# Layer 0 of a two-layer mixer: the transposed copy of x from a second load in runs of 32 channels, turned on VectorE

## The chip, the cores and the metric

The kernel runs on one core of a Trainium2 chip. The metric is device time in microseconds, the median of several runs. Beside the runs there is one profiled execution, from which all rows of the profile come; it has a time of its own. Engines are called PE (TensorE), DVE (VectorE), ACT (ScalarE), POOL (GpSimd) and SP (SyncE, whose queue issues nearly all DMAs here).

## The reference

The input x has 128 rows of 256 tokens of 256 channels, fp32. Two layers are applied, each to a group-normalised x (32 groups of 8 channels, mean and variance over all tokens), and added to x. Layer 0 is attention along the tokens of a row, with 8 heads of 32 channels, a bias b from a second input z that is the same for all rows, and a gate; layer 1 is attention with 4 heads within a band of 16 tokens. Cut to layer 0:

```python
g = _gn(x)                                   # group norm: mean and variance of each of 32 groups
m_norm = layer_norm(g)                       # over the channels of a token
q, k, v = m_norm @ Wq.T, m_norm @ Wk.T, m_norm @ Wv.T
b = (layer_norm(z) @ Wb.T)                   # one value per head and pair of tokens
gate = sigmoid(g @ Wg.T + bg)                # from g itself, not from m_norm
p = softmax(q @ k.T / sqrt(32) + b)
x = x + ((p @ v) * gate) @ Wo.T + bo
```

So layer 0 needs x twice with the channels on the partitions: as g for the gate, and as m_norm for q, k and v.

## The kernel before, in words

The work has three stages. The first reads all of x for the moments of the groups and all of z for the bias, whose exponential stays in SBUF (`eb`). It is a loop over 16 blocks of z with a hand-written plan (`plan`, `mark`) that slips the first steps of layer 0 in at quarters of blocks: `norm` makes the rows M0 and R0 (mean and reciprocal deviation of each channel, the same on all partitions) and centres pair 0, `weigh` takes its token moments, `now.turn` transposes it.

The second stage is layer 0, a loop over 64 pairs of rows; each pass handles steps of several pairs: `now` is in its scores, `nxt` is being prepared, `nn` is normalised, `was` and `old` are being finished. The third stage is layer 1, a loop over pairs as well.

Within a stage the order of each engine's instructions is the order in which they are written (`tc.manual_schedule()`), and each engine takes its own in order. Waits come from data and from buffers: pools with a number of buffers for each tag, PSUM tiles of the tag "s" (two buffers of 2 banks) for scores and for the transposes, and "mm" (two of one bank) for projections, values and output rows.

One pair passes through these steps; the lines are those of the profile:

- `__init__` (L1225, SP): loads xt, the pair with tokens on the partitions. It is made three pairs ahead.
- `centre` and `scale` (L1233, L1236, POOL): xg = (xt - M0) * R0, for `nn`.
- `moments`, `root`, `send`, `fetch` (L1246 to L1264): the layer norm's factor of each token, sent to DRAM in `rs_d` and fetched back as rs_r, a row repeated on all partitions.
- `turn` (L1274 on PE, L1278 on ACT): eight 128x128 transposes of xg into a PSUM tile of the tag "s", and two copies into xgT, channels on partitions.
- `normal` (L1283, POOL): xnT = xgT * rs_r. The layer norm's mean is taken out in the weights.
- `project` (L1296, L1300): gT from xgT (a tanh; the half that a sigmoid needs is in the weights), qT and kT from xnT. `values` (L1311, L1317): v from xnT.
- `scores` (L1330, L1337): keys times queries into two tiles of "s", and exp on ACT in place.
- `add_bias` (L1346 on DVE, L1351 on POOL): e = exp(scores) * eb, and the key sums eboth, which add the two halves of the keys.
- `apply` (L1362, L1370): e times v into ps_ov, and the sums of e into ps_su. `gate` (L1377): oT = (gT + 1) * ps_ov. `invert` (L1383 to L1391): 1/ps_su, sent to DRAM and fetched as rvb. `normalize` (L1407, POOL): oT * rvb.
- `out_row`, `keep_row` (L1417 to L1430): the output projection and the sum with xt; every four pairs eight rows of the new x go to DRAM, and their group moments for layer 1 are taken on DVE (L1445).

A pass of the loop has four rounds of scores. In the second, `nn` is scaled and gT of `now` is projected; in the third, `now.apply(0)` stands ahead of `nxt.turn()`, so that the transposes come between the sums (L1370) and `now.values(1)`; `nxt.normal()` follows the key sums of the third round on POOL. In the fourth round qT and kT of `nxt` are projected from xnT.

Layer 1 gets its transposed x in another way: a second load of x whose runs are 32 channels, four DMAs for a pair (L1720, xs), and one block transpose on DVE (L1730), then a bias on ACT (L1735).

Of the kernel before, what the change touches and what calls it, by code (L numbers as in the profile page):

```python
# [9 lines left out]
F32 = mybir.dt.float32  # L10
AF = mybir.ActivationFunctionType
ALU = mybir.AluOpType
# [4 lines left out]
P = 128  # L17
# [4 lines left out]
def bcast(ap, axis, n):  # L22

    ap = ap.unsqueeze(axis)
    shape = list(ap.shape)
    shape[axis] = n
    return ap.broadcast_to(shape)
# [746 lines left out]
def fast_kernel(  # L774
# [25 lines left out]
    nc = tc.nc  # L800
    S, I, C = x.shape
    CZ = z.shape[2]
    H = wbT.shape[1]
    D0 = C // H
# [3 lines left out]
    NB = I // P  # L808
    KC = C // P
    NP = S // 2  # L810
    N2 = 2 * I
# [4 lines left out]
    const = ctx.enter_context(tc.tile_pool(name="const", bufs=1))  # L816
    dram = ctx.enter_context(tc.tile_pool(name="dram", bufs=1, space=DRAM))

    ident = const.tile([P, P], F32, name="ident")
# [111 lines left out]
    for a in range(KC):  # L931
        for h in range(H1):
            n = P // H1
# [5 lines left out]
    for h in range(H1):  # L939
        n = P // H1  # L940
# [57 lines left out]
    def mm(name):  # L998
        return ps_mm.tile([P, 512], F32, name=name, tag="mm")
# [199 lines left out]
    HQ = P // D0  # L1199
    NT = 2 * NB  # L1200
# [11 lines left out]
    for n in range(RC):  # L1212
# [2 lines left out]
            bcast(ident.rearrange("p (q d) -> p q d", q=HQ)[:, :, n * D0 // RC], 2, D0),  # L1215
        )

    class Pair:


# [7 lines left out]
            )  # L1228


        def centre(self):
            self.xg = la.tile([P, NT, C], F32, name="xg", tag="xg", bufs=2)
            nc.gpsimd.tensor_tensor(self.xg, self.xt, bcast(M0, 1, NT), ALU.subtract)  # L1233

        def scale(self):
# [226 lines left out]
    def some(n):  # L1462
        for _ in range(min(n, len(later))):
            later.pop(0)()
# [10 lines left out]
    def pair(p):  # L1475
        return Pair(p) if p < NP else Nobody()
# [20 lines left out]
    def norm():  # L1497
        nonlocal M0, R0, nxt
        M0, R0 = next(steps)
        now.centre()  # L1500
        now.scale()
        nxt = pair(1)

    def weigh():
# [5 lines left out]

    plan = {
        (0, 4): begin, (1, 1): lambda: next(steps), (1, 3): lambda: next(steps), (1, 4): take, (2, 3): norm,
        (3, 4): weigh,
        (5, 3): lambda: now.send(nc.scalar),
# [13 lines left out]
    behind, nx, n = None, 0, 0  # L1528
# [39 lines left out]
    su = ps_o.tile([P, I], F32, name="ps_su")  # L1568

    with tc.manual_schedule():  # L1570
        old = was = Nobody()
        es = nn3 = None
        for p in range(NP):

            nxt.root()
            nxt.send()
            e0 = now.add_bias(0, 0, now.scores(0, 0))
            was.apply(1, es)
            was.gate(1)
            was.invert()  # L1580
            nxt.fetch()
            nn.centre()
            if p == 0:
                nxt.residual()
            now.project("qT", 1)
            now.project("kT", 1)
            some(1 if p < NP - 2 else 3)
            now.values(0)
            now.keep_values(0)

            es = e0, now.add_bias(0, 1, now.scores(0, 1))
            nn.scale()
            if p == 0:
                now.residual()
            for m in range(KC):
                now.project("gT", m)
            old.out_row(1)
            some(1 if p < NP - 2 else 3)
            old.keep_row(1)

            nn3 = pair(p + 3)
            e0 = now.add_bias(1, 0, now.scores(1, 0))
            now.apply(0, es)
            now.gate(0)
            nxt.turn()
            nxt.normal()
            was.normalize(0)
            now.values(1)
            now.keep_values(1)
            nn.moments(0)  # L1610
            if p == NP - 1:
                some(8)

            es = e0, now.add_bias(1, 1, now.scores(1, 1))
            was.normalize(1)
            nn.residual()
            nxt.project("qT", 0)
            nxt.project("kT", 0)
            nn.moments(1)
            some(3 if p < NP - 2 else 9)  # L1620
            was.out_row(0)
            was.keep_row(0)
            old, was, now, nxt, nn = was, now, nxt, nn, nn3
        was.apply(1, es)
        was.gate(1)
        was.invert()
        old.out_row(1)
        was.spread()
        old.keep_row(1)
        for r in range(2):  # L1630
            was.normalize_last(r)
        for r in range(2):
            was.out_row(r)
            was.keep_row(r)
        some(len(later))
# [29 lines left out]
    with tc.tile_pool(name="l1", bufs=2) as sb, tc.tile_pool(  # L1665
        name="l1s", bufs=4
    ) as sm, tc.tile_pool(name="ps1_mm", bufs=2, space=PSUM) as ps_mm, tc.tile_pool(
        name="ps1_s", bufs=1, space=PSUM
    ) as ps_s, tc.tile_pool(name="ps1_o", bufs=1, space=PSUM) as ps_o:

        def mm1(name):
            return ps_mm.tile([P, 512], F32, name=name, tag="mm")
# [174 lines left out]
        def pair1(p):  # L1847
            return Pair1(p) if p < NP else Nobody()
# [15 lines left out]
        with tc.manual_schedule():  # L1864
            now, nxt = pair1(0), pair1(1)
# [18 lines left out]
        with tc.manual_schedule():  # L1884
            was = Nobody()
            for p in range(NP - 1):
                nn = pair1(p + 2) if p == 0 else n3
# [27 lines left out]
                was, now, nxt = now, nxt, nn  # L1915
# [19 lines left out]
        ps = mm1("ok_ps")  # L1935
# [4 lines left out]
@with_exitstack  # L1940
def mixer_kernel(ctx, tc, *args):

    nc = tc.nc
    keep = ctx.enter_context(tc.tile_pool(name="verdict", bufs=1))
    verdict = keep.tile([1, 1], mybir.dt.int32, name="verdict")
    fast_kernel(tc, *args, verdict)
    again = nc.values_load(verdict[0:1, 0:1], min_val=0, max_val=1)
    with tc.If(again > 0):
        general_kernel(tc, *args)
# [53 lines left out]
```

## Time and profile before

| | |
|---|---|
| runs | 3310.61 us median of 3 (3309.5 to 3310.71) |
| profiled execution | 3316.03 us, its span 3314.3 us |
| busy, share of the span | PE 95%, DVE 64%, POOL 59%, ACT 44% |
| first stage | 0 to about 240 us |
| layer 0 | about 240 to 2090 us, PE busy 599.85 of the 600 us from 300 to 900 |
| layer 1 | from about 2098 us on |
| share of time that the DMA engines are busy | 0.23 from 300 to 900 us, 0.38 from 2110 to 3300 us |

The matmuls of PE overlap, and their ends are modelled, so a busy PE says less than the chain does: the chain of work that ended last is followed back from the last instruction, at each step to what released it, or to the instruction before it on its engine. Where it runs through one engine alone, that engine sets the pace there. An fp32 matmul appears as two records in most rows. A row of the timeline can stand for several instructions of one kind (xN), and its length is then from the first start to the last end.

### The profile page before, as it was taken

What the parts mean: (1) busy time and instruction counts of PE and PEld (TensorE: products, weight loads), DVE (VectorE), ACT (ScalarE), POOL (GpSimd) and SP (SyncE); (2) the same over time, 40 slices, a digit from 0 to 9 for tenths busy, and PEclk for the clock granted to TensorE, in tenths of its full rate; (3) what the DMA queues carried; (4) which work ended last, traced back from release to release, by engine and by line L of the source; (5) the groups of instructions that cost most, each with busy time, mean ns of one, the idle gap of its engine ahead of it and who ended that gap; (6) DMA issues with size and microseconds to landing.
All of it is one profiled execution on the core that took longest, in us unless ns stands there. A gap on an engine that the chain in (4) does not pass through costs nothing.

```text
span 3314.3 us, 80768 instructions
## 1 busy us (share of the span) xinstructions
PE 3157.9 (95%) x34656; PEld 1977.2 (60%) x34656; DVE 2121.6 (64%) x3179; ACT 1452.7 (44%) x2121; POOL 1962.8 (59%) x1375
## 2 busy tenths in 40 slices
PE   5389999999999999999999999699999999999998
PEld 3255555555555555555555555466666666666666
DVE  7955666666666666666666666466655555555566
ACT  2264444444444444444444444244444444444443
POOL 2378777777787777787887776233333333333332
PEclk8699999999999999999999999899999999999999
DMA  9951212212221222222122211533333434343431
GB/s 354 375 137 43 75 49 75 75 46 65 72 75 49 75 75 60 64 64 69 49 75 75 75 49 52 104 79 91 85 90 86 92 85 91 85 92 84 92 90 54
DMA packets 464879, 295.92 MB, mean 89 GB/s; under 512 B 312480, under 2 KB 413728, under 8 KB 463360
## 3 DMA queue, kind: packets, MB, share of 16 engines
q1 hardware_dynamic: 459440, 287.76, 31.7%
q8 instruction: 275, 4.51, 0.6%
q10 hardware_dynamic: 5072, 2.90, 0.3%
q14 instruction: 92, 0.75, 0.1%
HBM read 221.85 MB, written 68.75 MB: 88 GB/s over the span
## 4 chain that ended last, share of the span: by engine, by line
PE 91%; DVE 3%; DMA 3%; ACT 1%; POOL 1%; SPq 1%; issue 0%; ACTq 0%; POOLq 0%; DVEq 0%
PE ps_p L1296 21%; PE ps_p L1745 14%; PE ps_sc L1330 8%; PE ps_y L1833 7%; PE ps_ov L1362 7%; PE ps_v L1760 7%; PE ps_y L1417 7%; PE ps_v L1311 6%; PE ps_o L1802 3%; PE ps_su L1370 3%; PE ps_sc L1774 3%; PE ps_x L1274 2%; PE ps_su L1802 1%; DVE st L1178 1%; DVE zst L1103 1%; DMA zt<-in_z_dram 1%
## 5 line engine op out<-in xcount | busy, mean ns | idle before, releaser
L1351 POOL TENSOR_TENSOR eboth<-e 128x512 f32<-128x512 f32 x512 | 640.6, 1273 | 392.9 <-DVE e L1346 389.7
L1346 DVE TENSOR_TENSOR e<-ps_sc,eb 128x1024 f32<-128x1024 f32 x512 | 603.1, 1219 | 307.0 <-ACT ps_sc L1337 306.9
L1337 ACT ACTIVATE ps_sc<-ps_sc 128x1024 f32<-128x1024 f32 x512 | 492.8, 1006 | 509.2 <-PE ps_sc L1330 509.2
L1784 POOL TENSOR_TENSOR e<-e,bw 128x384 f32<-128x384 f32 x256 | 259.5, 1035 | 769.8 <-ACT e L1782 769.8
L1745 PE MATMUL ps_p<-xgT,w_in 128*128 128x512 f32 x1024 | 470.3, 602 | 4.5 <-issue 3.7
L1745 PEld LDWEIGHTS ps_p<-xgT,w_in 128*128 128x128 f32 x1024 | 190.1, 191 | 203.7 <-issue 174.8
L1330 PE MATMUL ps_sc<-qT,kT 32*128 32x256 f32 x4096 | 293.3, 400 | 2.1 <-ACT kT L1300 2.1
L1296 PE MATMUL ps_p<-xnT,wq 128*128 128x512 f32 x512 | 267.3, 634 | 3.5 <-POOL xnT L1283 3.1
L1833 PE MATMUL ps_y<-w_out,oT 128*128 128x256 f32 x1024 | 250.3, 388 | 2.6 <-DVE oT L1818 2.6
L1837 DVE TENSOR_TENSOR yo<-ps_y,xt 128x512 f32<-128x512 f32 x128 | 88.4, 690 | 251.9 <-PE ps_y L1833 149.7
L1362 PE MATMUL ps_ov<-e,v 128*32 128x256 f32 x4096 | 247.7, 382 | 0.0
L1417 PE MATMUL ps_y<-wo,oT 128*128 128x256 f32 x1024 | 242.1, 379 | 2.0 <-POOL oT L1407 1.2
L1417 PEld LDWEIGHTS ps_y<-wo,oT 128*128 128x128 f32 x1024 | 194.3, 190 | 82.5 <-issue 59.3
L1311 PE MATMUL ps_v<-wv,xnT 128*128 128x256 f32 x1024 | 242.2, 379 | 0.0
L1330 PEld LDWEIGHTS ps_sc<-qT,kT 32*128 32x128 f32 x4096 | 184.9, 184 | 94.4 <-issue 83.6
L1296 PE MATMUL ps_p<-xnT,wk 128*128 128x512 f32 x512 | 240.8, 592 | 0.0
L1296 PE MATMUL ps_p<-xgT,wg 128*128 128x512 f32 x512 | 236.8, 605 | 0.0
L1760 PE MATMUL ps_v<-w_in,xgT 128*128 128x256 f32 x1024 | 231.8, 379 | 0.0
L1815 DVE RECIPROCAL rv<-odd 128x256 f32<-128x256 f32 x128 | 224.4, 1753 | 4.4
L1760 PEld LDWEIGHTS ps_v<-w_in,xgT 128*128 128x128 f32 x1024 | 194.4, 190 | 53.5 <-issue 30.1
L1317 DVE TENSOR_TENSOR v<-ps_v,vb_r 128x512 f32<-128x512 f32 x128 | 88.6, 692 | 206.8 <-PE ps_v L1311 206.8
L1311 PEld LDWEIGHTS ps_v<-wv,xnT 128*128 128x128 f32 x1024 | 189.6, 190 | 50.8 <-issue 31.0
(169 smaller groups left out, 4989.9 us busy)
## 6 DMA issues: line engine op xcount, KB each, us to landing
xa<-in_x_dram SPq DMA_DIRECT2D x8, 4096.0 KB
xt<-in_x_dram SPq DMA_DIRECT2D x64, 512.0 KB
x<-xo SPq DMA_DIRECT2D x16, 2048.0 KB
xs<-x SPq DMA_DIRECT2D x256, 128.0 KB
xt<-x SPq DMA_DIRECT2D x64, 512.0 KB
rvb<-rsum SPq DMA_DIRECT2D x252, 128.0 KB
out_dram<-yo SPq DMA_DIRECT2D x63, 512.0 KB
zt<-in_z_dram SPq DMA_DIRECT2D x15, 2048.0 KB
```

Of the source, the lines that this page charges most:

```text
L1296: nc.tensor.matmul(ps, w[:, k, m * P : (m + 1) * P], getattr(self, src)[:, k, :], start=(k == 0), stop=(k == KC - 1),)
L1311: nc.tensor.matmul(self.ps_v[:, b * C : (b + 1) * C], self.xnT[:, k, t * P : (t + 1) * P], wv[:, k, :], start=(k == 0), stop=(k == KC - 1),)
L1330: nc.tensor.matmul(self.pss[q // 2][:, q % 2, b, :], self.kT[rs, c, r * I + b * P : r * I + (b + 1) * P], self.qT[rs, c, r * I : (r + 1) * I],
L1337: nc.scalar.activation(self.pss[a], self.pss[a], AF.Exp)
L1346: nc.vector.tensor_tensor(e, pss[a], eb[:, h : h + 2], ALU.mult)
L1351: nc.gpsimd.tensor_tensor(t, es[a][:, :, 0, :], es[a][:, :, 1, :], ALU.add)
L1362: nc.tensor.matmul(ov[q * D0 : (q + 1) * D0, c, :], self.v[:, r, b, h * D0 : (h + 1) * D0], es[q // 2][:, q % 2, b, :], start=(b == 0), st ...
L1417: nc.tensor.matmul(self.ps_y[:, b * C : (b + 1) * C], self.oT[r][:, k, b * P : (b + 1) * P], wo[:, k, :], start=(k == 0), stop=(k == KC - 1),)
L1745: nc.tensor.matmul(ps, w_in[:, k, n * C + m * P : n * C + (m + 1) * P], self.xgT[:, k, :], start=(k == 0), stop=(k == KC - 1),)
L1760: nc.tensor.matmul(ps[:, b * C : (b + 1) * C], self.xgT[:, k, t * P : (t + 1) * P], w_in[:, k, 2 * C : 3 * C], start=(k == 0), stop=(k == ...
L1784: nc.gpsimd.tensor_tensor(e[:, q], e[:, q], bcast(bw.rearrange("p b w -> p (b w)"), 1, KC), ALU.mult)
L1833: nc.tensor.matmul(ps[:, b * C : (b + 1) * C], self.oT[r][:, k, b * P : (b + 1) * P], w_out[:, k, :], start=(k == 0), stop=(k == KC - 1),)
```

## The change

Three things are different. The pair's transposed copy no longer comes from xg by PE but from a second load of x: `blocks` loads it with four DMAs on SP, each into 32 partitions, in runs of 32 channels (128 bytes), and `turn_blocks` turns it with two block transposes of 512 elements on DVE. Since this copy is neither centred nor scaled, `scale_blocks` does both on ACT, in place, with one scale and one bias for each channel; these stand in `col`, which `norm` makes once from R0 and M0 by four matmuls with one column of the identity. xg is still made, for the token moments, with one buffer instead of two. Pair 0 is still turned by PE.

The places in a pass: `nxt.turn_blocks()` and then `nn.blocks()` after the values of the first row, so ahead of the second round of scores; `nxt.scale_blocks()` after the projection of gT; and `nxt.normal()` at the head of the third round, ahead of the scores and their key sums, where it stood behind them. `now.gate(0)` keeps its place behind `apply(0)`, and now nothing stands between it and the values. The load for pair 1 is written ahead of the loop. In the built kernel the four DMAs of that first load do not stand together on SP: two of them are among the last loads of z.

```diff
@@ -1215,6 +1215,8 @@
             bcast(ident.rearrange("p (q d) -> p q d", q=HQ)[:, :, n * D0 // RC], 2, D0),
         )
 
+    col = const.tile([P, 2, KC], F32, name="col")
+
     class Pair:
 
 
@@ -1228,8 +1230,32 @@
             )
 
 
+        def blocks(self):
+
+            self.xs = la.tile([P, NB, KC, 2 * HQ, D0], F32, name="xs", tag="xs", bufs=1)
+            by_block = x[2 * self.p : 2 * self.p + 2].rearrange(
+                "s (i b n) (k j a) -> j b (n k) (s i) a", i=HQ, n=NB, k=KC, a=D0
+            )
+            for j in range(HQ):
+                nc.sync.dma_start(self.xs[j * D0 : (j + 1) * D0].rearrange("b n k i a -> b (n k) i a"), by_block[j])
+
+        def turn_blocks(self):
+            self.xgT = la.tile([P, KC, N2], F32, name="xgT", tag="xgT", bufs=2)
+            for n in range(NB):
+                nc.vector.transpose(
+                    self.xgT.rearrange("p k (s n i b) -> p n k s i b", s=2, n=NB, i=HQ)[:, n],
+                    self.xs[:, n].rearrange("p k (s i) a -> p k s i a", s=2),
+                )
+
+        def scale_blocks(self):
+            for k in range(KC):
+                nc.scalar.activation(
+                    self.xgT[:, k, :], self.xgT[:, k, :], AF.Identity,
+                    bias=col[:, 1, k : k + 1], scale=col[:, 0, k : k + 1],
+                )
+
         def centre(self):
-            self.xg = la.tile([P, NT, C], F32, name="xg", tag="xg", bufs=2)
+            self.xg = la.tile([P, NT, C], F32, name="xg", tag="xg", bufs=1)
             nc.gpsimd.tensor_tensor(self.xg, self.xt, bcast(M0, 1, NT), ALU.subtract)
 
         def scale(self):
@@ -1497,6 +1523,15 @@
     def norm():
         nonlocal M0, R0, nxt
         M0, R0 = next(steps)
+        ps = mm("ps_col")
+        for n, row in enumerate((R0, M0)):
+            for k in range(KC):
+                nc.tensor.matmul(
+                    ps[:, n * KC + k : n * KC + k + 1], row[:, k * P : (k + 1) * P], ident[:, 0:1],
+                    start=True, stop=True,
+                )
+        nc.vector.tensor_copy(col[:, 0], ps[:, 0:KC])
+        nc.vector.scalar_tensor_tensor(col[:, 1], ps[:, KC : 2 * KC], -1.0, col[:, 0], ALU.mult, ALU.mult)
         now.centre()
         now.scale()
         nxt = pair(1)
@@ -1568,6 +1603,7 @@
     su = ps_o.tile([P, I], F32, name="ps_su")
 
     with tc.manual_schedule():
+        nxt.blocks()
         old = was = Nobody()
         es = nn3 = None
         for p in range(NP):
@@ -1587,6 +1623,8 @@
             some(1 if p < NP - 2 else 3)
             now.values(0)
             now.keep_values(0)
+            nxt.turn_blocks()
+            nn.blocks()
 
             es = e0, now.add_bias(0, 1, now.scores(0, 1))
             nn.scale()
@@ -1594,16 +1632,16 @@
                 now.residual()
             for m in range(KC):
                 now.project("gT", m)
+            nxt.scale_blocks()
             old.out_row(1)
             some(1 if p < NP - 2 else 3)
             old.keep_row(1)
 
             nn3 = pair(p + 3)
+            nxt.normal()
             e0 = now.add_bias(1, 0, now.scores(1, 0))
             now.apply(0, es)
             now.gate(0)
-            nxt.turn()
-            nxt.normal()
             was.normalize(0)
             now.values(1)
             now.keep_values(1)
```

## The prediction

> **What bounds the kernel now.** I read three views in this order: the shares of the chain that ended last, that chain in order of time over one pair of layer 0, and the timeline of the same pair on the other engines. First the page's line on the chain:
>
> ```profile
> PE 91%; DVE 3%; DMA 3%; ACT 1%; POOL 1%; SPq 1%; issue 0%; ACTq 0%; POOLq 0%; DVEq 0%
> ```
>
> TensorE holds 91% of it. Inside layer 0 it holds all of it; the chain from 1216 to 1246 us (start, length, step):
>
> ```profile
> 1219.03 0.86 PE ps_su L1370 x16
> 1219.89 3.63 PE ps_p L1296 x8
> ...
> 1234.62 0.86 PE ps_su L1370 x16
> 1235.48 1.02 PE ps_x L1274 x8
> 1236.51 1.73 PE ps_v L1311 x8
> 1238.24 1.07 PE ps_sc L1330 x16
> 1239.31 3.82 PE ps_p L1296 x8
> 1243.13 1.73 PE ps_y L1417 x8
> ```
>
> The steps stand end to end. One pair is 4 scores (4.30), 2 applies with their sums (5.44), three projections (3.63+3.63+3.82), two values and two output rows (6.92) and the transposes (1.02): 28.76 us, the distance between two pairs. So what leaves TensorE here leaves the period, as long as nobody else comes late. Two things are seen besides. After ps_su the next group (ps_p at 1219.89) costs its ordinary 3.63, so ps_v will not pay for following ps_su directly. And the projection behind xnT takes 3.82 where its two sisters take 3.63: 0.19 is lost to a late operand. The waits from 300 to 2040 us name it (us in total, times, longest):
>
> ```profile
> PEld ps_p L1296 <- POOL xnT L1283: 66.0, 120, 0.9
> ...
> POOL xnT L1283 <- DMA rs_r<-rs_d: 0.6, 1, 0.6
> ```
>
> The other engines around the place of the change (start, busy, engine, line; the wait before it in brackets):
>
> ```profile
> 1225.29 0.69 DVE L1317 TENSOR_TENSOR v<-ps_v,vb_r 128x512 f32<-128x512 f32 x1 [2.15 <-PE ps_v L1311]
> ...
> 1227.47 2.36 DVE L1346 TENSOR_TENSOR e<-ps_sc,eb 128x1024 f32<-128x1024 f32 x2 [1.49 <-ACT ps_sc L1337]
> ...
> 1230.51 0.37 SPq L1264 DMA_DIRECT2D rs_r<-rs_d  x1
> 1231.29 2.37 POOL L1236 TENSOR_TENSOR xg<-xg,R_l 128x1024 f32<-128x1024 f32 x1
> 1231.61 1.15 PE L1330 MATMUL ps_sc<-qT,kT 32*128 32x256 f32 x16
> ...
> 1232.79 1.93 ACT L1337 ACTIVATE ps_sc<-ps_sc 128x1024 f32<-128x1024 f32 x2 [2.11 <-PE ps_sc L1330]
> 1233.90 2.36 DVE L1346 TENSOR_TENSOR e<-ps_sc,eb 128x1024 f32<-128x1024 f32 x2 [1.49 <-ACT ps_sc L1337]
> ...
> 1235.27 2.51 POOL L1351 TENSOR_TENSOR eboth<-e 128x512 f32<-128x512 f32 x2 [1.61 <-DVE e L1346]
> ```
>
> Each of them has idle time exactly where the change puts work.
>
> **What the Trainium skill says.** (1) TensorE: Matmul & The Clock Gate, Part 4: PE-mode transpose, gives some 275 ns for one transpose in a kernel. The trace's median for L1274 is 273 ns, but they overlap: eight take 1.02 on the chain, so the duration isn't the cost. (2) VectorE: DVE Perf Modes, The three transpose paths: VectorE turns 32x32 blocks only, SBUF to SBUF. The trace agrees: layer 1 does so at L1730, from a load whose runs are already 32 channels. (3) Vector Engine (DVE) Microarchitecture Reference, 3.8 The reshape front-end and per-opcode configuration: one element per cycle and lane. At 0.96 GHz 1024 elements are 1.07 us; the trace has 1.234, so 0.17 is fixed. (4) DMA: Bandwidth & Descriptors, Queues, rings and completion order: on each engine descriptors are consumed in ring order. So loads queued behind rs_r do not hold it up; no run here isolates that.
>
> **The change, part by part, for one pair.** TensorE: eight transposes go, 1.02. xnT is made earlier, so the third projection costs 3.63: 0.19 more. That is 1.20 (28.76 less the sum without rounding, 27.56). Now who could be late.
>
> VectorE: two block transposes of 512 elements between L1317 and L1346. Each is an estimate from L1730 and page (3): 0.53 + 0.17 = 0.70; two are 1.40. Below: 1.23, half of L1730 each; above: 2.47, each as dear as a whole L1730, in case the output in pieces of 128 runs worse. I take 1.40. L1317 ends at 1225.98 and L1346 starts at 1227.47: 1.49 idle covers it. Without that cover L1346 and POOL's eboth slip, and TensorE notices only when the scores at 1231.61 find their PSUM tile unread: L1346 ends at 1229.83, another 1.78 of slack. Even 2.47 costs nothing.
>
> ScalarE: two copies of 0.589 (L1278) go, two in-place scalings come, 0.69 to 0.72 each by L1300 and L1735. They move ahead of the exp at 1232.79. The last gT ends at 1230.68, so they end at 1232.1: 0.7 before the exp.
>
> POOL: the two xnT products (L1283, 2.51) move ahead of one pair of key sums. The scaling of xg ends at 1233.66, and xgT is ready at 1232.1. If rs_r has landed, xnT runs to 1236.2, the key sums to 1238.7 (0.9 later; their first reader is ps_su at 1247.6), and the product with rvb (L1407) to 1239.9, where its reader ps_y now starts at 1242.97-1.20=1241.8. xnT's own reader starts at 1238.2: two spare. POOL's work stays 23.4 us, 85% of the shorter period.
>
> rs_r: queued 1230.51, behind rvb. Nothing in layer 0 shows its landing; from both sides: at least 1.7 us (the last rsum, queued 2058.44, lets rvb go at 2060.14), at most 7.2 (at 1237.73 it had landed). With rvb's 512 KB and its own 256 KB at some 350 GB/s (the page's first two slices show 354 and 375), 2.2 us from 1228.70, plus 1.7: 1232.6 is my estimate, in time for 1233.66.
>
> SP and DMA: four loads of 128 KB a pair, issue 0.83 each (median of L1720), right after rs_r, so ahead of the next xt and of the store of x. They wait for the block transposes, done at 1227.4, when SP arrives at 1230.9. SP is then held till 1234.2; behind it xt is issued some 2 us later, is read at about 1250, and the next send is at 1248. Their time on the engines: layer 1 is 38% busy in a pair of 18.39 us, 7.0 us, of which its other 1.05 MB need 3.0 at 350 GB/s; the rest, 4.0, bounds the loads. Layer 0 goes from 23% to (6.6+4.0)/27.56 = 38%. The data has 23 us to land.
>
> PSUM: scores at 1238.17 now start 1.02 earlier, 1237.15, and need the e before them read, 1236.26: 0.9 to spare. This is the tightest one.
>
> Ahead of the loop: four matmuls for col (like L1692's, 1.9 for the group) lie in the z stage, whose chain is TensorE and ScalarE there: 0 to 1.9, taken 1.0. VectorE waits for them, behind L990, and has 3.66 idle soon after. Of the four loads for pair 1 one stands in SP's order where DMA idles (165 to 175 us), one between z loads where it is full: 1.0, with 0 and 4.0 as ends. The first pair gains more, 2.5: TensorE waited there till 261.86 for an xnT that stood behind key sums of 2.5.
>
> **Sum.** 62 x 1.20 + 2.5 - 1.0 - 1.0 = 74.9. The profiled execution took 3316.03 (span 3314.3): 3241.1. The median of the runs is 5.42 below that execution, so 3310.61 - 74.9 = 3235.7. The last pairs and layer 1 stay.
>
> **Rivals.** *Late scale factors, slower.* xnT now stands before the key sums and L1407, so POOL, in order, waits for rs_r with all of them behind. L1407 ends 6.3 after xnT may start (2.5+2.5+1.3), and ps_y wants it at 1241.8. It costs nothing while rs_r lands by 1235.5, 5.0 after its issue; it eats the gain at 6.2. At the upper end, 7.2, it loses 2.2 against a gain of 1.2: 62 x 1.0 = 62 more, some 3372. For it: the landing is unseen. Against: rsum's 1.7, and the xs loads come behind it.
>
> *Another wait takes the place.* The 0.9 at the scores is used up, by scalings that reach into the exp or by transposes of over 3.3 us. With half of the gain gone it is 3310.6 - 62 x 0.6, about 3273. Against: it needs two of my margins to fail.
>
> *No change.* If TensorE's pace were set by a loop through POOL (85%), the period would stay: 3311. Against: L1351 waits 389.7 us in all for VectorE's e, so POOL isn't behind.
>
> **Chances.** Forecast 0.80, within 3228 and 3243 (seams of 0.1 a pair either way, and the ends of the prologue's costs). Partial gain 0.10, no change 0.03, slower 0.07. The range 3227 to 3265 leaves out half of the partial case, the last two and a little below. About 0.2% is what a measurement of this kernel can tell from no change: faster 0.89, same 0.04, slower 0.07.
>
> **What will show it.** Right: ps_x is gone from the loop, all three projections take 3.63, the distance of pairs is 27.56, the transposes take about 0.70 and L1346 waits less but still for ScalarE. Wrong: xnT waits for rs_r, ps_y for L1407, scores for L1346, or transposes of over 1.6 us each.

## The result, and the profile after

The changed kernel takes 3331.78 us (median of 4 runs, 3325.77 to 3334.63) against 3310.66 us for the kernel before beside it (4 runs): a ratio of 1.0058, 95% interval 1.004 to 1.0077. It is slower by 0.6%, where 3235.7 us was forecast. Its profiled execution took 3325.77 us, with a span of 3324.0 (before: 3316.03 and 3314.3). That is the fastest of its four runs, while the profiled execution of before took longer than each of its four; so the two profiles show only 9.7 us of the 21.1 between the medians.

Where these 9.7 us lie: the first scores of layer 0 start at 244.6 instead of 240.3 us (+4.3); from there to the first load of layer 1 it takes 1866.2 instead of 1858.1 us (+8.1); layer 1 to the end takes 1213.2 instead of 1215.9 us (-2.7). So the loop of layer 0, which was to become some 77 us shorter, became 8 us longer. The page's line on the chain that ended last shows that TensorE no longer holds layer 0 alone:

```profile
PE 69%; DMA 10%; DVE 10%; POOL 5%; issue 2%; ACT 2%; SPq 2%; ACTq 0%; POOLq 0%; DVEq 0%
```

It was PE 91% and POOL 1%. From 300 to 900 us PE is busy 584.73 of 600 us, where it was 599.85. The chain of the changed kernel over the stretch that the prediction showed (start, length, step) tells both what went as planned and what did not:

```profile
1214.82 1.27 POOL xnT L1309
1216.09 2.27 POOL eboth L1377 x2
...
1218.50 1.28 POOL oT L1433
...
1219.83 1.99 PE ps_y L1443 x8
...
1240.35 0.86 PE ps_su L1396 x16
1241.22 1.92 PE ps_v L1337 x8
1243.14 1.08 PE ps_sc L1356 x16
1244.22 3.63 PE ps_p L1322 x8
```

The transposes (ps_x) are gone and the third projection costs 3.63 instead of 3.82. But the chain comes out of POOL: TensorE's output row (ps_y) waits for oT (L1433, the product with rvb), which stands behind the key sums (L1377), which stand behind xnT (L1309). And ps_v right behind ps_su takes 1.92, not 1.73. The waits from 300 to 2040 us of the changed kernel (us in total, times, longest) name the head of this queue:

```profile
POOL xnT L1309 <- DMA rs_r<-rs_d: 187.2, 60, 4.7
...
PEld ps_y L1443 <- POOL oT L1433: 82.2, 60, 1.7
...
PE ps_y L1443 <- POOL oT L1433: 33.1, 48, 0.8
```

Before, xnT waited for rs_r once, for 0.6 us. Now it waits in every pair, 3.1 us in the mean. Two of the signs that the prediction had named for being wrong are there: xnT waits for rs_r, and ps_y for the product with rvb.

### The profile page after: what moved, and what is told of

It reads as the page before. It is cut to its first block, busy times and chain, and to the rows that moved or that the text cites. A ratio compares the mean times of both kernels' runs of the same rounds, so it can differ in the third digit from the quotient of the medians.

```text
span 3324.0 us, 80098 instructions
## 1 busy us (share of the span) xinstructions
PE 3118.4 (94%) x34160; PEld 1922.1 (58%) x34160; DVE 2229.1 (67%) x3307; ACT 1473.2 (44%) x2121; POOL 1958.2 (59%) x1375
## 4 chain that ended last, share of the span: by engine, by line
PE 69%; DMA 10%; DVE 10%; POOL 5%; issue 2%; ACT 2%; SPq 2%; ACTq 0%; POOLq 0%; DVEq 0%
PE ps_p L1783 14%; PE ps_p L1322 11%; PE ps_y L1871 7%; PE ps_v L1798 7%; PE ps_y L1443 6%; PE ps_sc L1356 6%; DMA rsum<-rv 4%; PE ps_ov L1388 4%; PE ps_v L1337 4%; PE ps_o L1840 3%; DVE e L1372 3%; PE ps_sc L1812 3%; DMA rs_r<-rs_d 2%; PE ps_su L1396 2%; POOL oT L1433 2%
## 5 line engine op out<-in xcount | busy, mean ns | idle before, releaser
L1377 POOL TENSOR_TENSOR eboth<-e 128x512 f32<-128x512 f32 x512 | 639.3, 1271 | 207.9 <-DVE e L1372 205.6
L1322 PE MATMUL ps_p<-xnT,wq 128*128 128x512 f32 x512 | 262.4, 626 | 16.4 <-POOL xnT L1309 13.2
L1309 POOL TENSOR_TENSOR xnT<-xgT,rs_r 128x512 f32<-128x512 f32 x128 | 159.7, 1268 | 197.1 <-DMA rs_r<-rs_d 197.1
```

The costliest lines, as they stand in the source:

```text
L1322: nc.tensor.matmul(ps, w[:, k, m * P : (m + 1) * P], getattr(self, src)[:, k, :], start=(k == 0), stop=(k == KC - 1),)
L1377: nc.gpsimd.tensor_tensor(t, es[a][:, :, 0, :], es[a][:, :, 1, :], ALU.add)
```

## Where the time came from: a loop that closes on itself

Two views of one pair of the changed kernel show it. First SP's queue (start, time in the queue, line):

```profile
1226.80 0.36 SPq L1285 DMA_DIRECT2D rs_d<-lrs  x1
1228.61 0.54 SPq L1410 DMA_DIRECT2D rsum<-rv  x1
1235.41 1.71 SPq L1417 DMA_DIRECT2D rvb<-rsum  x4
1237.23 0.37 SPq L1290 DMA_DIRECT2D rs_r<-rs_d  x1
...
1254.67 0.37 SPq L1285 DMA_DIRECT2D rs_d<-lrs  x1
```

The factors are sent at 1226.80. rvb can go only when rsum has landed, 6.8 us after rsum's issue; rs_r is issued behind rvb. Then POOL (start, busy, line, the wait before it in brackets):

```profile
1241.46 2.50 POOL L1309 TENSOR_TENSOR xnT<-xgT,rs_r 128x512 f32<-128x512 f32 x2 [2.07 <-DMA rs_r<-rs_d]
1243.92 2.49 POOL L1377 TENSOR_TENSOR eboth<-e 128x512 f32<-128x512 f32 x2
1246.37 1.27 POOL L1433 TENSOR_TENSOR oT<-oT,rvb 128x512 f32<-128x512 f32 x1
1247.60 2.49 POOL L1377 TENSOR_TENSOR eboth<-e 128x512 f32<-128x512 f32 x2
1250.05 1.27 POOL L1433 TENSOR_TENSOR oT<-oT,rvb 128x512 f32<-128x512 f32 x1
1251.28 2.39 POOL L1265 TENSOR_TENSOR xt<-xt,bo_r 128x1024 f32<-128x1024 f32 x1
1253.62 1.02 POOL L1282 TENSOR_TENSOR lrs<-lrs,mhalf 128x4 f32<-128x4 f32 x1
```

From xnT to the root of the *next* pair (L1282) POOL works without a gap, and the next send leaves at 1254.67: 13.21 us after xnT began. So there is a ring: send, queue, rs_r, xnT, 13.2 us of POOL, next send. Its length is the time from a send to its xnT plus 13.2. Here 14.66 + 13.21 = 27.87, and 1254.67 - 1226.80 = 27.87. For the pair before this one the same views give 15.02 from the send to xnT (1198.57, 1213.59) and 13.21 more to the next send, 28.23. Whoever is late in this ring is late for the next pair as well: nothing gives the time back while the ring is longer than TensorE's own work.

In the kernel before, the same two views show more room. SP's queue:

```profile
1220.06 0.36 SPq L1259 DMA_DIRECT2D rs_d<-lrs  x1
...
1248.82 0.36 SPq L1259 DMA_DIRECT2D rs_d<-lrs  x1
```

POOL:

```profile
1237.73 2.51 POOL L1283 TENSOR_TENSOR xnT<-xgT,rs_r 128x512 f32<-128x512 f32 x2
...
1247.77 1.02 POOL L1256 TENSOR_TENSOR lrs<-lrs,mhalf 128x4 f32<-128x4 f32 x1
```

The send is at 1220.06 and xnT at 1237.73, 17.7 us later, but it is only 11.1 us from there to the next send (1248.82). xnT was then started by the end of the key sums (1235.27 + 2.51), with rs_r landed: it was issued 10.45 after the send, and with the 4.2 us that it takes from issue to xnT in the change, the ring had about 3 us to spare. The change moved xnT ahead of a pair of key sums (2.5 us), so it starts earlier, waits for rs_r, and has so much more of POOL's work between itself and the next send.

The medians over the pairs of layer 0, read in the timelines of SP and POOL of each run's one profiled execution, in us after the send:

| run | send to rvb | send to rs_r's issue | send to xnT | distance of pairs | time, us | ratio (95%) |
|---|---|---|---|---|---|---|
| before | 9.12 | 11.11 | 17.68 | 28.77 | 3310.66 | |
| after | 9.12 | 11.55 | 15.82 | 28.92 | 3331.78 | 1.0058 (1.004 to 1.0077) |
| e1, xnT back behind the key sums | 9.64 | 11.54 | 18.02 | 28.76 | 3321.07 | 1.0014 (1.0007 to 1.0021) |
| e2, root and send early | 9.93 | 11.96 | 16.80 | 27.75 | 3255.64 | 0.982 (0.9803 to 0.9836) |
| e3, rs_r ahead of rsum and rvb | 13.88 | 8.70 | 13.79 | 27.75 | 3257.13 | 0.9824 (0.9807 to 0.984) |
| e4, loads last in the pass | 9.74 | 12.23 | 17.13 | 30.34 | 3415.2 | 1.03 (1.0283 to 1.0317) |
| e5, send in runs of 16 bytes | 4.43 | 6.26 | 13.37 | 27.76 | 3250.67 | 0.9782 (0.9766 to 0.9798) |
| e8, before with the new order alone | 9.96 | 12.01 | 16.98 | 30.17 | 3404.57 | 1.0257 (1.024 to 1.0274) |
| e9, the change again | 10.01 | 12.80 | 16.78 | 29.98 | 3402.92 | 1.0252 (1.023 to 1.0274) |
| e10, as e4 | 10.01 | 12.41 | 17.65 | 30.87 | 3441.8 | 1.0362 (1.0344 to 1.0379) |
| e11, e2 with e5 and e7 | 7.85 | 9.68 | 16.79 | 27.75 | 3245.33 | 0.9772 (0.9756 to 0.9789) |
| e12, before with e2's edit | 10.08 | 12.47 | 21.09 | 28.77 | 3316.17 | 0.9984 (0.9977 to 0.9991) |

In the five runs in which the ring is closed (after, e4, e8, e9, e10), the time from send to xnT plus 13.2 is 29.0, 30.3, 30.2, 30.0 and 30.9; the distance of pairs is 28.9, 30.3, 30.2, 30.0 and 30.9.

In any kernel the time from send to xnT and the time from xnT to the next send add up to the distance. What marks these five is that the second time is POOL's 13.2 us of work without a gap in each of them, and that xnT waits for rs_r in all pairs or nearly all; in the other runs of the table it lies between 7.7 and 14.4, and xnT waits less or not at all. The sum alone doesn't show that the ring sets the pace; the runs that open it (e1, e2, e3, e5) do.

The later runs with the small send have a longer round trip, and the kernel before takes 3316 to 3321 us beside them; so each time is compared only with the kernel before that ran next to it. e1 to e4 ran on chip 2, e5 to e8 on chip 13 and e9 to e12 on chip 1; which chip the first two ran on is not known, so the chip and the occasion can't be told apart.

## The experiments

**e1_norm_back: xnT back where it stood.**

```diff
-            nxt.normal()
             e0 = now.add_bias(1, 0, now.scores(1, 0))
             now.apply(0, es)
             now.gate(0)
+            nxt.normal()
```

> Everything of the change stays, but xnT is made where it stood before: behind the key sums of the third round (L1377) on POOL. Loop theory (xnT, standing early, closes a loop: send of rs_d, then rvb, then rs_r, then xnT and the 13.2 us of POOL work up to the next send, 28.9 us in all): with xnT behind the key sums the loop has 2.5 us less of POOL behind rs_r, so it no longer sets the pace, and xnT waits for no rs_r. But xnT then ends where it ended before, so TensorE arrives 1.0 earlier and waits for it: 3303 to 3318, no gain and no loss against before. Rival (the traffic of the second load is what delays rs_r, wherever xnT stands): stays at 3325 or more.

Measured: 3321.07 against 3316.39 us, 3 us above the range expected, pairs 28.76 apart, and no wait for rs_r. The loss is all but gone, and so is the gain: the projection of TensorE now waits for xnT (119 weight loads, 113.3 us in all). The transposes of PE are gone and the pair is as long as before, so the eight of them alone are worth nothing while xnT stands behind the key sums.

**e2_root_early: the ring opened at POOL.** Root and send no longer stand at the end of POOL's queue but ahead of the last product with rvb and of the residual.

```diff
+        nxt.root()
+        nxt.send()
         for p in range(NP):
-            nxt.root()
-            nxt.send()
...
             es = e0, now.add_bias(1, 1, now.scores(1, 1))
+            nn.moments(1)
+            nn.root()
+            nn.send()
             was.normalize(1)
             nn.residual()
...
-            nn.moments(1)
```

> The changed kernel, with root and send of rs_d taken ahead of the last product with rvb and of the residual on POOL, at the end of the pass before instead of the head of the next. Loop theory: 1.27 + 2.38 = 3.65 us of POOL leave the loop, 28.9 becomes 25.3, less than TensorE's 27.56, so TensorE sets the pace: 3310.7 - 62 x 1.2 + 4 for the longer first stage, 3236 to 3250, and no wait of xnT for rs_r. Rival (rs_r is late because the loads of xs crowd it): the wait stays at some 2 us a pair and the time above 3290.

Measured: 3255.64 us, 1.8% faster than before, though some 6 us above the range expected. xnT starts even later after its send than in the change (16.80), yet the pairs are 27.75 apart, because less of POOL's work stands between xnT and the next send. rs_r is hardly waited for:

```profile
POOL xnT L1309 <- DMA rs_r<-rs_d: 11.2, 14, 2.6
```

The loop of layer 0 takes 1792.1 us, 66.0 less than before. The pair stays 0.19 above the forecast's 27.56, the seam of ps_v. The transposes, the scalings and the second load are all in it, so none of them was the trouble.

**e3_fetch_first: the ring shortened at SP.** `nxt.fetch()` is written ahead of `was.invert()`, so rs_r is issued ahead of rsum and rvb.

```diff
+            nxt.fetch()
             was.invert()
-            nxt.fetch()
```

> The changed kernel, with the fetch of rs_r written ahead of the two steps of invert on SP, so that rs_r waits for the landing of rs_d alone and not for rsum and rvb. Loop theory: rs_r is issued about 9 us after the send instead of 11.5, has rvb's 512 KB no longer ahead of it, and lands some 12 after the send instead of 15.8; the loop falls under 27.56: 3238 to 3260. If instead the product with rvb, now later by some 3 us, takes over as the last to come, the time lies between 3260 and 3310 and ps_y waits for L1433. Rival (crowding by xs): the wait for rs_r stays, above 3300.

Measured: 3257.13 us, the same gain by another part of the ring: rs_r goes 8.70 after the send and xnT starts at 13.79; 13.79 + 13.2 = 27.0 is below 27.75. rs_r is waited for in 29 pairs, 21.4 us in all. In these pairs xnT starts 4.19 us after rs_r's issue, and over all pairs 4.95, against 4.21 in the change: rs_r comes no sooner although rvb's 512 KB no longer go ahead of it. What this edit wins is the earlier issue.

**e4_blocks_late: the rival, that the four loads behind rs_r hold it up.**

```diff
             nxt.turn_blocks()
-            nn.blocks()
...
             was.keep_row(0)
+            nn.blocks()
```

> The changed kernel, with the four loads of xs issued at the end of the pass, so that they no longer follow right behind rs_r on SP's queue. Loop theory: loads that stand behind rs_r do not hold it up, so its landing stays at some 4.2 us after its issue and the time within 3320 to 3340; it may get worse if the loads now stand just ahead of rs_d. Rival (the loads crowd rs_r): the landing falls to about 2 us, the wait of 3.1 a pair shrinks by 2, and the time falls under 3290.

Measured: 3415.2 us. The rival falls: with the loads out of the way rs_r takes no less from its issue to xnT (4.80 us in the pairs that wait, against 4.21 in the change; in e8 below, which has no second load at all, it takes 4.59). The ring theory had not foreseen 3415 either. Two more runs settle what this is: **e9_change_again** is the change itself beside **e10_blocks_late_again**, the same kernel as e4.

> The changed kernel once more, unaltered, to stand beside the next run on one chip. The loop consists of DMA round trips, and the runs so far differ in them: from send to rvb 9.1 us in the first profile of the change, 9.5 to 10.2 in later runs. If the loop sets the pace, the changed kernel takes up each such microsecond 62 times, so it may now lie anywhere from 3325 to 3410, with the distance of pairs equal to xnT's start after the send plus 13.2. If something else set its pace, it is again 0.6% above before.

> The loads of xs at the end of the pass, once more, on the chip of e9. If their place behind rs_r costs nothing and their place ahead of rs_d costs something, this one is slower than e9 by 20 to 90 us; if the 3415 of the first time was that chip's slower round trip, the two are within 10 us of each other.

Measured: the change takes 3402.92 us here (1.0252), not 3331.78, and the late loads 3441.8, 39 us more. So of the 121 us by which the late loads lose on this occasion, 82 are the change's own, at a longer round trip: send to xnT is 16.78 instead of 15.82. That is 0.96 a pair; the distance of pairs grew by 1.06, and 62 x 1.06 = 66 of the 71 us by which the change is slower here than the first time. The kernel before, whose ring has room, moved by only 10 us between the same two occasions. Why the round trip is longer there is not settled; it is so in every kernel with the small send that ran later, e12 among them (10.08 from send to rvb), and on all three chips. Nor is it settled why rs_r comes 0.65 us later still when the loads come late (4.98 against 4.33 in these two runs).

**e5_wide_send: the ring shortened at the DMA.** The 512 factors are written to DRAM in the order (partition, block of tokens), so that each partition writes one run of 16 bytes instead of four of 4 bytes. POOL's product reads them back with a stride.

```diff
-            queue.dma_start(rs_d[self.p].rearrange("(t p) -> p t", p=P), self.rs)
+            queue.dma_start(rs_d[self.p].rearrange("(p t) -> p t", p=P), self.rs)
...
-                nc.gpsimd.tensor_tensor(self.xnT[:, k, :], self.xgT[:, k, :], self.rs_r, ALU.mult)
+                nc.gpsimd.tensor_tensor(
+                    self.xnT[:, k, :].rearrange("q (t p) -> q t p", t=NT),
+                    self.xgT[:, k, :].rearrange("q (t p) -> q t p", t=NT),
+                    self.rs_r.rearrange("q (p t) -> q t p", t=NT), ALU.mult,
+                )
```

> The changed kernel, with xnT early and root where the change has it, but rs_d laid out so that the send writes 16 bytes a partition (128 runs instead of 512 of 4 bytes); POOL reads rs_r with a stride of 4 elements instead. Loop theory: from send to rvb it takes 9.1 us before and after the change, whether rsum is queued 1.8 or 2.8 behind the send, so it is the 512 small writes that hold the queue; a quarter of them takes 2 to 5 us out of that, the loop falls under TensorE's 27.75 and the time to 3250 to 3265 (before on the chip at 3311 to 3316). If the round trip is mere latency of a write to DRAM, send to rvb stays at 9 and the time above 3315. A slower POOL with the strided operand would show as a longer L1309.

Measured: 3250.67 us, 2.2% faster than before, and xnT never waits for rs_r. SP's queue of this kernel for one pair:

```profile
1213.51 0.33 SPq L1285 DMA_DIRECT2D rs_d<-lrs  x1
1216.16 0.54 SPq L1414 DMA_DIRECT2D rsum<-rv  x1
1217.92 1.71 SPq L1421 DMA_DIRECT2D rvb<-rsum  x4
1219.73 0.37 SPq L1290 DMA_DIRECT2D rs_r<-rs_d  x1
```

rvb goes 1.76 us after rsum, where it went 6.80 after it in the change: the small writes of the send had held rsum up. The traces' DMA records and semaphores tell in what way. In the pair of the changed kernel shown above, the packets of the send lie between 1227.5 and 1228.5 and those of rsum between 1229.8 and 1230.0; then no packet moves until rvb is issued at 1235.41. What is late is the completion on which SP waits. The send's last one comes at 1235.16, rsum's at 1235.40. In the median the send completes 8.5 us after its issue in the change, and 1.4 us after it here. So the small writes don't keep the DMA engines busy over this time; they are reported as done late, and rsum behind them. Why they complete so late isn't shown. POOL's product takes 1557 ns instead of 1268 and that costs nothing.

**e6_values_before_apply: the 1.92 us of ps_v.** On top of e2, the values of the second row are put ahead of the apply, so that they follow scores and not ps_su.

```diff
+            now.values(1)
             now.apply(0, es)
...
-            now.values(1)
```

> The kernel with root early (e2), with the values of the second row put ahead of the first apply, so that ps_v no longer follows ps_su directly. If the 0.19 us that ps_v takes more in the changed kernel (1.92 against 1.73) is the price of that seam, ps_v is back at 1.73, the period falls from 27.75 to 27.56 and the time by 12 us to some 3243. If the scores that now follow ps_su pay the same, nothing changes: 3255.

Measured: 3258.16 us, nothing gained. The chain of this kernel:

```profile
1234.49 1.08 PE ps_sc L1356 x16
1235.57 1.92 PE ps_v L1337 x8
```

The 0.19 us came along: ps_v pays behind ps_sc as well. It takes 1.73 behind a projection and, in the kernel before, behind the transposes. There the transposes themselves stood behind ps_su, so they may have paid in its place: in e8, where they stand behind a projection, the eight take 0.87 on the chain, not 1.02.

**e7_col_late: the first stage.** On top of e2, the four matmuls for `col` and the two steps of DVE are moved from `norm` to the end of `weigh`.

```diff
     def norm():
         M0, R0 = next(steps)
-        ps = mm("ps_col")
...
+        ps = mm("ps_col")
...
```

> The kernel with root early (e2), with the four matmuls for col and their two VectorE steps put some blocks of z later, where R0 and M0 are long done. In the changed kernel TensorE stands 2.64 us waiting for R0 there, and the first scores come 4.3 us later than before. If that wait is the cause, the first scores come 3 us earlier and the time falls to some 3252; if it is the second load of x among the loads of z, only 1 us or less.

Measured: 3254.54 us, first scores at 245.0 instead of e2's 245.5. A miss by most of what was expected. In the eight other kernels that have the change and small writes the first scores start at 244.6 (the change) to 250.2 us (e6), without the change at 240.3 to 241.9 (before, e8, e12), and with the change and the wide send at 240.9 (e5) and 235.2 us (e11). Each of these is one profiled execution. So some of it seems to hang on the send, and the 4.3 us are not pinned to `col`; their cause stays open.

**e8_order_only: the kernel before with the new order and nothing else.** TensorE still transposes, there is no second load; only `turn` and `normal` stand where the change puts their successors.

```diff
+            nxt.turn()
...
+            nxt.normal()
             e0 = now.add_bias(1, 0, now.scores(1, 0))
...
-            nxt.turn()
-            nxt.normal()
```

> The kernel before, with its transposes on TensorE and no second load; only the order is that of the change: the transposes stand behind the projection of gT, xnT ahead of the third round and its key sums. Loop theory: xnT waits for rs_r in nearly every pair, some 2 to 4 us, and the period is set by the loop at 28.5 to 29.3 instead of by TensorE: 3300 to 3345, though nothing was added. Rival (the second load is what makes rs_r late): no such wait, the 0.19 behind xnT is won, 3299 to 3305.

Measured: 3404.57 us, pairs 30.17 apart. The mechanism is the one expected; the loss is larger, as the wait (4.4 us in the mean) and the distance lie above their ranges and the time 60 us above its own. This settles which part of the change makes it slow: the new order is enough, without the second load, and e1 narrows it to the place of xnT on POOL. The chain of this kernel runs through the ring itself:

```profile
1210.81 8.05 DMA rsum<-rv
...
1220.70 4.84 DMA rs_r<-rs_d
...
1226.90 1.27 POOL xnT L1283
```

rsum needs 8.05 us and rs_r 4.84, and between them stand rvb's four issues. xnT waits for rs_r 55 times, 241.0 us in all.

**e11_both: root and send early (e2), the wide send (e5) and `col` late (e7) together.**

> The changed kernel with root early, col late and the send of rs_d in runs of 16 bytes: all margins together. TensorE sets the pace at 27.75 a pair without exceptions: 62 x 1.02 us less than before, a ratio of 0.977 to 0.981, as good as e5 or e7 and not better, and xnT waits for rs_r in no pair.

Measured: 3245.33 us, 0.9772 of the kernel before, the lowest of all, though not to be told from e5's 0.9782; it beats both kernels. The pairs stay 27.75 apart, since TensorE now sets the pace; nothing is left in the ring to win.

**e12_before_root_early: e2's edit in the kernel before.** It was to tell whether the early root is a gain of its own, without the change.

> The kernel before, with root and send early and nothing else. Its pace is TensorE's, and xnT is made after rs_r has long landed, so an earlier send gives nothing: within 0.2% of before. A gain here would say that the loop already mattered before the change.

Measured: 3316.17 against 3320.92 us, 0.9984 (0.9977 to 0.9991), pairs 28.77 apart. The ring had room there, so opening it is worth 5 us, 0.16%, inside the 0.2% that was expected. What e2 gains comes from the change, once it is let through.

## Why the prediction was wrong, point by point

- **"It costs nothing while rs_r lands by 1235.5, 5.0 after its issue."** This is the step that failed. It holds the issue of rs_r fixed at 1230.51 and lets only the landing move. But the residual and the next root stand behind xnT on POOL, so what is late here makes the next send late, with it rsum, rvb and the next rs_r. The condition comes from the ring: xnT may start 27.56 - 13.2 = 14.4 us after the send, rs_r is issued 11.1 after it, so it has 3.2 us to land, not 5.0. A landing of 4.2, which the limit of 5.0 would have let pass for nothing, is 1.0 too late, and 11.1 + 4.2 + 13.2 is a period of 28.5 (28.92 measured). The trace of before held all of this but the landing: the order of POOL, the send behind the root, the issue 10.45 us after the send (1220.06 to 1230.51).
- **"1232.6 is my estimate", 2.1 us after the issue.** rs_r takes 4.2 us in the change (the pairs range from 3.45 to 5.47). So the estimate was half of the measured time, though inside the bounds given, 1.7 and 7.2. The lower bound had been read from the last rsum, which has no send ahead of it; in the ring rsum takes 7.2 us in the median of the change (6.8 in the pair shown, 8.05 in that of e8). The prediction asked what stands behind rs_r on SP's queue, and not what stands ahead of rsum.
- **The rival "Late scale factors, slower"** was the right mechanism and place, with a chance of 0.07. Its price was wrong: 62 us at a landing of 7.2. In truth every us by which the ring is longer than TensorE's work is carried on from pair to pair, so 15.82 + 13.2 gives 29.0 at a landing of 4.2.
- **"POOL's work stays 23.4 us, 85%", so POOL isn't behind.** True and beside the point: POOL is busy 471 of 600 us and waits in every pair. A share of busy time doesn't see a ring that is made of work and waits.
- **"ps_v will not pay for following ps_su directly."** It does: 1.92. The reason given was that ps_p costs its ordinary 3.63 behind ps_su. But each ps_p of a pair stands behind ps_su or ps_sc, so there was no other ps_p to compare with. The kernel before had shown the right row in its last pair, where no transposes stand between (its chain from 2066 us on):

```profile
2070.11 0.86 PE ps_su L1370 x16
2070.97 1.94 PE ps_v L1311 x8
```

  So TensorE's period is 27.75, not 27.56: 62 x 0.19 = 12 us of the forecast's gain. By e8, not all of the 1.02 us was the transposes' own: behind a projection the eight take 0.87. The Trainium skill, TensorEngine Tiling (Array Packing), Tiling Modes, Key Properties, says that a change of the tiling mode drains TensorE. The runs fit that, as ps_sc and ps_su use parts of the array (32 rows, 32 columns; 32*128 and 128*32 in the profile's rows) and ps_v all of it (128*128): 1.92 behind ps_sc and ps_su, 1.73 behind ps_p. The page gives no price; here it is 0.19 us. That the drain is the cause was not isolated.
- **VectorE and ScalarE** were right. The transposes take 0.68 each (forecast 0.70), the scalings 0.80 each (forecast 0.69 to 0.72), and the multiplication behind them still waits for ScalarE, by 0.28. The timeline of the changed kernel:

```profile
1231.63 1.29 DVE L1245 STREAM_TRANSPOSE xgT<-xs 128x512 f32<-128x512 f32 x2
1233.20 2.35 DVE L1372 TENSOR_TENSOR e<-ps_sc,eb 128x1024 f32<-128x1024 f32 x2 [0.28 <-ACT ps_sc L1363]
...
1236.31 1.51 ACT L1252 ACTIVATE xgT<-xgT,col 128x512 f32<-128x512 f32 x2
```

- **SP, DMA and PSUM** were right in the main: the share of the DMA engines is 0.35 (forecast 0.38), xs is never waited for, and no scores wait for PSUM. The four issues hold SP for 4.1 us in the median, not 3.3.
- **"First pair 2.5", "1.0" and "1.0" ahead of the loop** give +0.5 in all. The first scores start 4.3 later; the four matmuls for `col` alone left TensorE idle for 2.64 us ahead of them, waiting for R_l. As e7 shows, they are not the whole cause.
- **The sum.** With the ring opened (e2), the gain is 1792.1 against 1858.1, 66.0 us in the loop, where the steps gave 62 x 1.20 + 2.5 = 76.9; the seam of ps_v, 12 us, accounts for the 11 missing. But for that seam the sum for TensorE was sound; what was not is the claim that TensorE would set the pace.

## What to carry to other kernels

When a step is moved ahead on an in-order engine and waits for a DMA there, follow its result all the way round to the next instance of what it waits for: if that send stands behind the step on the same engine, add up the ring (queue, landing, work to the next send) and compare it with the period. A limit for a wait that takes the issue as fixed is wrong in a ring, for a delay is carried from pass to pass. If the ring is too long, put the root and the send ahead of the work that doesn't need them, issue the fetch first, or write it in longer runs: each of the three alone was enough here.

## What the runs showed of the hardware that was not expected

- 512 writes of 4 bytes hold up what is queued behind them, though their packets are through within some 1 us. They complete 8.5 us after their issue in the change, and rvb, which waits for the rsum behind them, goes 9.1 us after the send (to 10.3 in later runs). With 128 writes of 16 bytes, the same 2 KB, it is 1.4 and 4.4 us (e5). The Trainium skill, DMA: Bandwidth & Descriptors, Specifications, says that transfers below 512 bytes are not at line rate. Both sends here lie below 512 bytes, so that line alone doesn't tell them apart. Whether the size of a write or the number of writes makes the difference isn't isolated.
- A row of 2 KB fetched onto 128 partitions takes 4.2 us from issue to use in the change (median of the pairs that wait; 4.3 in e9). Nothing that was taken out of its way made it shorter: 4.2 in the pairs of e3 that wait, 4.95 in all of them, without rvb's 512 KB ahead of it; 4.8 and 5.0 without the four loads behind it (e4, e10); 4.6 without any second load (e8).
- The round trip differed by about 1 us between runs of the same kernel (after and e9). Chip and occasion aren't told apart here. The kernel before, with slack in its ring, differed by 0.3% between the two occasions, the change by 2.1%.
- POOL's product with one operand read at a stride of 16 bytes takes 1557 ns, against 1268 ns in order.
